# Square roots by logarithm and exponential, and a rotation whose sums TensorE makes while it transposes

## The chip, the cores and the metric

The kernel runs on one core of a Trainium2 chip, as one launch. The core has five engines that run their own instruction streams beside each other and wait for one another by semaphores: TensorE (PE, with its weight loads listed as PEld), VectorE (DVE), ScalarE (ACT), GpSimd (POOL) and SyncE (SP, which here issues transfers). Sums of matmuls are kept in PSUM, everything else in SBUF. The metric is the time of one launch on the device in microseconds (us), as the median of several runs. A profile is taken of one execution; its length is told by the span, from its first to its last instruction.

## What is computed

The reference is a network of four blocks of three layers on a small sequence x (2 batches of 128 rows, 256 wide) with a longer context (2 batches of 2048 rows). Every layer begins with a layer norm and ends with a residual sum:

```python
x = x + _L0_xattn_ref(_layernorm(x), ctx, ...)   # softmax attention over the context
x = x + _L0_attn_ref(_layernorm(x), ...)         # gated scan
x = x + _L0_ffn_ref(_layernorm(x), ...)          # mixture of 16 experts
...                                              # L1: cross attention, linear attention, soft mixture
x = x + _L2_xattn_ref(_layernorm(x), ctx, ...)   # linear attention with a sigmoid gate
...                                              # L2: rotary attention, mixture of low-rank experts
x = x + _L3_xattn_ref(_layernorm(x), ctx, ...)   # 16 heads over 2048 + 128 keys, RMS norm, rotary
x = x + _L3_attn_ref(_layernorm(x), ...)         # state-space layer
x = x + _L3_ffn_ref(_layernorm(x), ...)          # gated feed-forward with 4-bit weights
```

Two pieces matter here. The first is 1/sqrt(v + eps): in `_layernorm`, in the RMS norms of two layers and in an L2 norm. The second is the state-space layer L3_attn, with 64 heads and a state of N = 128:

```python
Bm = rmsnorm((x @ WB.T).reshape(B_, L, H, N), Bn_w) + B_bias      # Cm likewise
theta_cumsum = jnp.cumsum(theta * dt[..., None], axis=1)          # 64 angles for each head and row
Bm = rope(Bm, theta_cumsum); Cm = rope(Cm, theta_cumsum)          # x0*c - x1*s, x0*s + x1*c
...
h = a_t * h + b_t * outer(B_prev, x_prev) + g_t * outer(B_t, x_t) # scan over rows
y_t = C_t . h
```

The kernel makes the scan from products: C Bᵀ of each head (128 x 128), weighted by decays, times x.

## The kernel before

The kernel is one program of stages, a function for each layer. In most stages each operation is recorded through a small helper, `InOrder` (L219 to L227), which keeps the instructions of an engine in the order in which the program text calls them; therefore very many instructions of the profile show one line, L227, and are told apart by the names of their tiles.

**Roots.** `rstd` (L148 to L151) makes 1/sqrt(scale*v + eps) with two instructions, Sqrt on ScalarE and a reciprocal on VectorE. `norm_rows` and `layernorm` (L153 to L168) call it; `rooted` of the third block's cross attention (L1512) and `rooted` of the state-space layer (L1894) write out the Sqrt, and `rotated` (L1515) and `scaled` (L1897) the reciprocal; `l1_ffn` does it for the L2 norm (L1028). ScalarE's functions stand in tables, of which one set is active at a time; where the next function isn't in it, an instruction ACT_TABLE_LOAD stands ahead of it. Sqrt, Exp, Sin, Sigmoid and Gelu alternate all through the kernel. In l2 the gate of the cross attention is a Sigmoid (L1219) and is multiplied with 1/den later (L1268). `Tables.finish` (L313), called at L2239, takes the sines and cosines of the rotary angles of l3_xattn.

**l3_xattn** (L1430 on) goes through 8 groups of heads; keys and queries are normed and rotated by VectorE for the next group while TensorE makes the scores S and the products py of the present one.

**l3_attn** goes through 16 rounds: 8 groups of 8 heads by 2 batches. A round has, in the order in which its data flow: `angles` (projection `pt`), `stepped` (`td`, VectorE), `summed_angles` (sum over rows by a triangular matmul, TensorE), `reduced_angles` (a cast on ScalarE and a subtraction: `sc`), `sines` (Abs and two Sin, ScalarE), `decays` (`lm`, `ex`), `projected` (B and C as `pb`, two PSUM tiles of 128 x 1024, and their squares in `bc`), `squares` (two sums, `rs`), `rooted`, `scaled` (16 ScalarE multiplications `bc` <- `pb`, `rs`, one for B or C and head), `biased` (norm weight `nw` and bias `bb`: four VectorE operations of 128 x 1024), `rotated` (six VectorE operations of 128 x 1024: `t`, `ro`, `ro`, twice), `turned` (16 transposes of 128 x 128 on TensorE into four PSUM tiles, each then copied to `rT` by ScalarE), `products` (C Bᵀ, two times four matmuls), `decayed` (`m1` on VectorE, `m2` on GpSimd), `mixed` (32 matmuls with 32 columns of weights), `gated` (VectorE).

The rounds are pipelined by hand: step n of the loop at L2008 runs `decays` to `scaled` of round n, `biased` to `turned` of round n-1, `products` to `mixed` of round n-2, `gated` of round n-3 and the angles of round n+1. The order on each engine is that of the text. For one step it is

- TensorE: decays, pb (16), products of the first four heads, pt, products of the other four, angle sums, transposes, mixed;
- VectorE: bc (nw), bc (bb), gated, bc (nw), bc (bb), t, ro, ro, t, m1, ro, td, ro, m1, squares (2), reciprocal, lm, sc;
- ScalarE: a table load, ex (2), squares (2), Abs, a load, Sin (2), a load and a one-element Sqrt (`warm`, L2057), rT (4), Sqrt, cast, the 16 multiplications.

All matmuls of the layer but `pb` share four PSUM tiles (L1720). The last round is done in two halves of four heads, so `turned` is called twice there. Weights of the coming groups are fetched by SP (`weights`, L1732); the pool of single weights, `w4`, has three buffers (L2249), one each for `wx`, `wz` and, at the end, Wout.

Of the kernel before, what the change touches and what calls it, by code (L numbers as in the profile page):

```python
# [22 lines left out]
P = 128  # L23
# [12 lines left out]
class Net:  # L36


    def __init__(self, ctx, tc, ins):
# [6 lines left out]
        self.act = ctx.enter_context(tc.tile_pool(name="act", bufs=1, reuse_waits="tile"))  # L46

        c = self.const
        self.x = c.tile([P, B, D], F32, name="x")
# [90 lines left out]
    def copy(self, out, in_):  # L140
# [4 lines left out]
        else:  # L145
            self.nc.vector.tensor_copy(out, in_)

    def rstd(self, out, in_, scale, eps, act=None):  # L148
        nc = self.nc
        (act or nc.scalar).activation(out, in_, AF.Sqrt, bias=eps, scale=scale)  # L150
        nc.vector.reciprocal(out, out)  # L151

# [10 lines left out]

    def layernorm(self):
        xn = self.act.tile([P, B, D], F32, tag="xn", name="xn")
        for b in range(B):
            self.norm_rows(xn[:, b, :], self.x[:, b, :])
        return xn  # L168
# [111 lines left out]
class Tables:  # L280
# [32 lines left out]
    def finish(self):  # L313
        act = self.g.nc.scalar
        act.activation(self.cos, self.sin, AF.Abs)
        act.activation(self.cos, self.cos, AF.Sin, bias=self.g.half_pi, scale=-1.0)
        act.activation(self.sin, self.sin, AF.Sin)


# [378 lines left out]
def l0_attn(g):  # L698
# [6 lines left out]
    with tc.tile_pool(name="l0a", bufs=2, reuse_waits="tile") as p:  # L705
# [7 lines left out]
        for dc in range(2):  # L713
            ps = g.mm([P, 2, T])
            pg = g.mm([P, T])
            sl = slice(dc * P, (dc + 1) * P)
            g.project(ps[:, 0, :], lambda c: wi[:, c, sl], lambda c: xnT[:, c, :])
            g.project(ps[:, 1, :], lambda c: wf[:, c, sl], lambda c: xnT[:, c, :])
            g.project(pg, lambda c: wg[:, c, sl], lambda c: xnT[:, c, :])
            gate = p.tile([P, T], F32, tag="gate", name="gate")  # L720
            act.activation(gate, ps[:, 1, :], AF.Sigmoid)
            nc.gpsimd.memset(gate[:, P:P + 1], 0.0)
            om = p.tile([P, T], F32, tag="om", name="om")
            act.activation(om, ps[:, 1, :], AF.Sigmoid, scale=-1.0)
            v = p.tile([P, T], F32, tag="v", name="v")
            act.activation(v, ps[:, 0, :], AF.Sigmoid)
            nc.vector.tensor_tensor(v, v, ps[:, 0, :], ALU.mult)
            nc.vector.tensor_tensor(v, v, om, ALU.mult)
            o = p.tile([P, T], F32, tag="o", name="o")
            nc.vector.tensor_tensor_scan(o, gate, v, 0.0, ALU.mult, ALU.add)  # L730
            nc.gpsimd.tensor_tensor(osq[:, dc, :], o, o, ALU.mult)
            sg = p.tile([P, T], F32, tag="sg", name="sg")
            act.activation(sg, pg, AF.Sigmoid)
            if dc:
                g.mixing.decays(act)
            nc.vector.tensor_tensor(sg, sg, pg, ALU.mult)
            nc.vector.scalar_tensor_tensor(yT[:, dc, :], o, gn[:, dc:dc + 1], sg, ALU.mult, ALU.mult)
# [134 lines left out]
def l1_mixing(g, ctxT):  # L872
# [6 lines left out]
    with tc.tile_pool(name="l1x", bufs=2, reuse_waits="tile") as p:  # L879
        mix, dd = g.mixing, g.mixing.dd  # L880
        act = InOrder(tc, nc.scalar)

        def normed(b, n):
# [104 lines left out]
def l1_ffn(g, mu, b1):  # L988
# [6 lines left out]
    with tc.tile_pool(name="l1f", bufs=2, reuse_waits="tile") as p:  # L995
# [21 lines left out]
        for b in range(B):  # L1017
# [9 lines left out]
            nc.scalar.activation(xu[:, b, :], xl[:, b, :], AF.Square, accum_out=n2)  # L1027
            nc.scalar.activation(n2, n2, AF.Sqrt)  # L1028
            nc.vector.tensor_scalar(n2, n2, 1e-12, None, ALU.max)
            nc.vector.reciprocal(n2, n2)  # L1030
            nc.vector.tensor_scalar(xu[:, b, :], xl[:, b, :], n2, sc, ALU.mult, ALU.mult)
# [84 lines left out]
        def hidden(ep):  # L1116
# [7 lines left out]
            nc.vector.tensor_tensor(hv, ph[:, :, :, 0:H], rz.unsqueeze(3).to_broadcast([P, 2, B, H]), ALU.mult)  # L1124
            nc.scalar.activation(hv, hv, AF.Gelu)

# [23 lines left out]
def l2(g, ctxT, codes, last):  # L1150
# [9 lines left out]
    with tc.tile_pool(name="l2", bufs=1, side="right", reuse_waits="tile") as p:  # L1160
# [8 lines left out]
        wkv, wq, wg = (g.load("L2_xattn_" + k) for k in ("Wkv", "Wq", "Wg"))  # L1169
        bg = mine("bg", [P, 2], g.ins["L2_xattn_bg"], pc)  # L1170
        wxo = mine("wxo", [P, 2, D], g.ins["L2_xattn_Wo"], pc)
        wqk, wv, wo = (g.load("L2_attn_" + k) for k in ("Wqk", "Wv", "Wo"))
# [33 lines left out]
        def context_attention(px, b):  # L1206
# [11 lines left out]
            for dc in range(2):  # L1218
                nc.scalar.activation(gate[:, dc, :], ps[:, 1, dc, :], AF.Sigmoid, bias=bg[:, dc:dc + 1])  # L1219
            yield  # L1220
# [36 lines left out]
            den = px.tile([P, 2, P], F32, tag="den", name="den", bufs=1)  # L1257
            nc.vector.tensor_scalar(den, pn[:, 1], 1e-6, None, ALU.add)
            pk = g.mm([P, 2, P])
# [6 lines left out]
            for c in range(2):  # L1266
                nc.tensor.matmul(pn[:, 0, c, :], lhsT=kvb[:, c, :], rhs=q[:, c, :], start=True, stop=True)
            nc.vector.tensor_tensor(den, den, gate, ALU.mult)  # L1268
            oT = px.tile([P, 2, P], F32, tag="oT", name="oT", bufs=1)
# [160 lines left out]
def l3_xattn(g, ctxT, cos, sin, values):  # L1430
# [12 lines left out]
    with ExitStack() as ctx:  # L1443
# [18 lines left out]
        class Group:  # L1462
# [49 lines left out]
            def rooted(self, lo, hi):  # L1512
                act.activation(self.rs[:, lo:hi], self.rs[:, lo:hi], AF.Sqrt, bias=g.eps6, scale=1.0 / HD)

            def rotated(self, lo, hi):  # L1515

                kq, rot, b = self.kq, self.rot, self.b
                n = hi - lo
                dve.reciprocal(self.rs[:, lo:hi], self.rs[:, lo:hi])
                dve.tensor_tensor(kq[:, lo:hi, :], kq[:, lo:hi, :], self.rs[:, lo:hi].unsqueeze(2).to_broadcast([P, n, HD]), ALU.mult)  # L1520
# [191 lines left out]
def l3_attn(g):  # L1712
# [5 lines left out]
    with tc.tile_pool(name="l3w", bufs=2, reuse_waits="tile") as pw, tc.tile_pool(name="l3a", bufs=1, reuse_waits="tile") as p, tc.tile_pool(name="l3t", bufs=2, reuse_waits="tile") as p2, \  # L1718
            tc.tile_pool(name="l3aps", bufs=1, space=PSUM, reuse_waits="tile") as g.ps:
        def mm(shape=(P, 512)):  # L1720
            return g.ps.tile(list(shape), F32, tag="mm", name="mm", bufs=4)
# [6 lines left out]
        nc.sync.dma_start(nw, g.ins["L3_attn_BCn_w"].partition_broadcast(P))  # L1728

        late = p.tile([P, 4, P], BF16, name="late")  # L1730
        nc.vector.memset(late, 0.0)
# [94 lines left out]
        class Round:  # L1826
# [67 lines left out]
            def rooted(self):  # L1894
                act.activation(self.rs, self.rs, AF.Sqrt, bias=g.eps6, scale=1.0 / N)

            def scaled(self, parts=(slice(0, HG),)):  # L1897
                dve.reciprocal(self.rs, self.rs)
                for hs in parts:
# [9 lines left out]
            def rotated(self, hs=slice(0, HG)):  # L1909

                nh = hs.stop - hs.start
                e1, e2 = self.bc[:, :, hs, 0:64], self.bc[:, :, hs, 64:128]
                sb, cb = (self.sc[:, i, hs].unsqueeze(1).to_broadcast([P, 2, nh, 64]) for i in range(2))
                if hs.start == 0:
                    self.ro = p2.tile([P, 2, HG, N], F32, tag="ro", name="ro", bufs=1)
                r1, r2 = self.ro[:, :, hs, 0:64], self.ro[:, :, hs, 64:128]
                for r, x, y, op in ((r1, e1, e2, ALU.subtract), (r2, e2, e1, ALU.add)):
                    t1 = p2.tile([P, 2, HG, 64], F32, tag="t1", name="t1", bufs=1)[:, :, 0:nh, :]
                    dve.tensor_tensor(t1, y, sb, ALU.mult)
                    yield  # L1920
                    dve.tensor_tensor(r, x, cb, ALU.mult)
                    yield
                    dve.tensor_tensor(r, r, t1, op)
                    yield

            def turned(self, halves=(0, 1)):
                if 0 in halves:
                    self.rT = p2.tile([P, 2, HG, P], F32, tag="rT", name="rT")
                for n in halves:
                    for a in range(2):  # L1930
                        tp = mm([P, 4, P])
                        for i in range(4):
                            pe.transpose(tp[:, i, :], self.ro[:, a, 4 * n + i, :], g.ident)
                        act.copy(self.rT[:, a, 4 * n:4 * n + 4, :], tp)
# [42 lines left out]
        halves = (slice(0, HG // 2), slice(HG // 2, HG))  # L1977
        warm = g.sm([P, 1], "warm")
        rounds = {n: Round(*todo[n]) for n in range(2)}
# [20 lines left out]
        reduced = second.reduced_angles()  # L2000
        next(reduced)
        first.sines()
        first.decays()
        second.decay_inputs()
# [3 lines left out]
        for n in range(1, len(todo) + 3):  # L2008
# [47 lines left out]
            if now:  # L2056
                act.activation(warm, g.eps6, AF.Sqrt)  # L2057
            if rot and n - 1 < last:
# [81 lines left out]
def l3_ffn(g, codes, out):  # L2140
# [4 lines left out]
    with tc.tile_pool(name="l3sc", bufs=1, reuse_waits="tile") as psc, tc.tile_pool(name="l3f", bufs=1, reuse_waits="tile") as p, tc.tile_pool(name="l3d", bufs=2, reuse_waits="tile") as p2, \  # L2145
# [27 lines left out]

        xn = g.layernorm()
        tp = g.ps.tile([P, 2, B, P], F32, tag="up", name="tp", bufs=3)
# [40 lines left out]
def tile_perceiver(ctx: ExitStack, tc: tile.TileContext, ins, out: bass.AP):  # L2216
# [3 lines left out]
    with tc.tile_pool(name="w", bufs=1, reuse_waits="tile") as g.w, tc.tile_pool(name="ctxT", bufs=1, reuse_waits="tile") as pc, tc.tile_pool(name="l3t", bufs=1, reuse_waits="tile") as pt, \  # L2220
# [4 lines left out]
        with g.psum():  # L2225
            with tc.tile_pool(name="l1s", bufs=1, reuse_waits="tile") as pm:
# [4 lines left out]
                with tc.tile_pool(name="beside", bufs=1, reuse_waits="tile") as tmp:  # L2231
                    slots, tables = Slots(g, pm, tmp), Tables(g, pt, tmp)
                    ex = gate_spread(g, tmp)
                    l0_attn(g)
                    l0_ffn(g, itertools.chain(slots.steps(), [None] * 6, tables.steps()), ex)
                l1_mixing(g, ctxT)
                mixed.close()
                l1_ffn(g, slots.mu, slots.b1)
            tables.finish()  # L2239
            codes = Codes(g, ctx.enter_context(tc.tile_pool(name="codes", bufs=1, side="right", reuse_waits="tile")))  # L2240
# [7 lines left out]
    with tc.tile_pool(name="w_end", bufs=1, reuse_waits="tile") as g.w:  # L2248
        g.w_bufs = {"w2": 1, "w4": 3, "row": 1}  # L2249
        l3_attn(g)  # L2250
# [126 lines left out]
```

## Time and profile before

| | |
|---|---|
| median of 3 runs | 1529.2 us (1528.87 to 1530.35) |
| the profiled execution | 1534.16 us |
| its span | 1532.4 us |
| mean granted clock of TensorE | 0.917 |
| busy: PE, DVE, ACT, POOL | 1389.1, 1121.8, 812.5, 141.3 us |
| l3_xattn, about | 700 to 1130 us |
| rounds of l3_attn | from about 1150 to 1460 us, 19.2 us each in the steady part |
| table loads shown at L227 | 72, 1283 ns each |

Two numbers of time stand side by side: the profiled execution took 1534.16 us, of which the span covers 1532.4, and the runs without a profile have a median of 1529.2. A line of groups reads: line, engine, operation, tile written <- tiles read, shape, count | busy time in all, mean ns of one | idle time of the engine just before them, and what ended it. A line of the timeline reads: start, length, engine, line, operation, tiles, shape and count. A line of the chain reads: start, length, what the end was waiting for then. Matmuls overlap: the length of one record is longer than the distance from one to the next.

### The profile page before, as it was taken

How to read it: one execution, taken by the hardware profiler on the slowest of the kernel's cores; microseconds unless marked ns; L12 is line 12 of the kernel's file. 1: busy time of each engine (PE TensorE's matmuls, PEld its weight loads, DVE VectorE, ACT ScalarE, POOL GpSimd, SP SyncE). 2: the span in 40 equal slices, each digit the busy share in tenths (PEclk: the TensorE clock that was granted, in tenths of full speed). 3: DMA queues.
4: the chain of work that ended last, by engine and by line, in shares of the span. 5: the costliest groups of instructions: out<-in, count | busy, mean ns of one | idle time of the engine just before them, and what ended most of it. 6: DMA issues, size and time to landing. Idle time of an engine off the chain costs nothing.

```text
span 1532.4 us, 18453 instructions
## 1 busy us (share of the span) xinstructions
PE 1389.1 (91%) x6936; PEld 852.2 (56%) x6936; DVE 1121.8 (73%) x1970; ACT 812.5 (53%) x1251; POOL 141.3 (9%) x140
## 2 busy tenths in 40 slices
PE   8859997799989999989999999999888999999878
PEld 5413333677456786655666656665444555555557
DVE  6889997576256476675776776777537999999876
ACT  3567776333232433353554455455448888888721
POOL 6620001011000000000000000000000111111110
PEclk9955555999999999989999999999999999999989
DMA  7799999754250342412001000000152222221110
GB/s 189 137 177 204 204 201 197 222 167 146 75 170 9 96 139 65 121 42 69 29 0 55 29 6 37 28 28 0 36 198 81 92 96 97 96 97 42 35 35 7
DMA packets 225140, 143.87 MB, mean 94 GB/s; under 512 B 177897, under 2 KB 203770, under 8 KB 220699
## 3 DMA queue, kind: packets, MB, share of 16 engines
q1 hardware_dynamic: 221696, 140.75, 35.4%
q10 hardware_dynamic: 3290, 1.77, 0.5%
q8 instruction: 55, 0.90, 0.2%
q0 software_dynamic: 64, 0.18, 0.1%
q14 instruction: 35, 0.28, 0.1%
HBM read 90.33 MB, written 8.65 MB: 65 GB/s over the span
## 4 chain that ended last, share of the span: by engine, by line
PE 55%; DVE 27%; ACT 9%; DMA 4%; issue 3%; POOL 2%; DVEq 0%; SPq 0%; ACTq 0%; POOLq 0%
PE mm L184 9%; PE wide L227 9%; PE py L227 8%; DVE S L227 7%; PE mm L227 6%; PE tr L227 5%; DVE bc L227 4%; DVE ro L227 4%; DMA pT<-Si 2%; ACT bc L227 2%; PE acc L1235 2%; PE sc L227 2%; PE acc L227 2%; DVE t L227 1%; DVE rs L227 1%
## 5 line engine op out<-in xcount | busy, mean ns | idle before, releaser
L227 DVE TENSOR_SCALAR_CACHE_REDUCE S<-sc 128x1024 f32<-128x1024 f32 x128 | 150.4, 1219 | 6.9 <-PE sc L227 3.6
L227 PE MATMUL py<-pT,v 128*128 128x512 f32 x272 | 141.1, 605 | 9.5 <-ACT pT L227 9.5
L227 PE MATMUL sc<-kT,qT 48*128 48x512 bf16 x256 | 130.0, 614 | 19.7 <-DMA kT<-kpad 6.5
L227 ACT ACTIVATE Si<-S,nb,sq 128x4096 int16<-128x4096 f32 (+1 forms) x35 | 122.7, 3506 | 42.8 <-issue 27.8
L227 ACT COPY pT<-tr 128x512 f32<-128x512 f32 x136 | 78.7, 584 | 82.7 <-PE tr L227 82.7
L227 PE MATMUL wide<-kT,qT 128*128 128x512 f32 x256 | 116.7, 599 | 0.0
L227 ACT ACTIVATE S<-S,nb 128x2176 f32<-128x2176 f32 x32 | 67.5, 2108 | 92.5 <-DVE nb L227 92.5
L227 PE MATMUL pb<-wb,xT 128*128 128x512 f32 x256 | 112.6, 592 | 0.0
L227 PEld LDWEIGHTS tr<-ident,S 128*128 128x128 f32 x544 | 67.5, 141 | 68.4 <-issue 37.7
L227 DVE TENSOR_SCALAR_CACHE_REDUCE S<-wide 128x1024 f32<-128x1024 f32 x64 | 77.7, 1223 | 27.9 <-PE wide L227 27.5
L227 ACT ACT_TABLE_LOAD x72 | 92.4, 1283 | 3.2 <-PE mm L227 1.2
L227 PEld LDWEIGHTS <-pT 128*128 128x128 bf16 x1024 | 36.5, 105 | 94.7 <-issue 87.8
L227 PE MATMUL tr<-ident,S 128*128 128x128 f32 x544 | 81.4, 274 | 3.4 <-ACT S L227 3.3
L227 PEld LDWEIGHTS pb<-wb,xT 128*128 128x128 f32 x256 | 48.9, 191 | 59.9 <-issue 55.6
L227 PEld LDWEIGHTS wide<-kT,qT 128*128 128x128 f32 x256 | 47.4, 193 | 50.4 <-issue 43.6
L227 ACT ACTIVATE bc<-pb,rs 128x128 f32<-128x128 f32 x256 | 67.8, 424 | 0.9 <-DVE rs L227 0.9
L227 ACT ACTIVATE bc<-pb 128x1024 f32<-128x1024 f32 x32 | 32.8, 1025 | 49.3 <-PE pb L227 49.3
L184 PE MATMUL mm<-wvs,ctxT 128*128 128x512 f32 x116 | 57.0, 614 | 0.0
L227 PE MATMUL wide<-w,ctxT 128*128 128x128 f32 x448 | 53.0, 277 | 2.6 <-DVE S L227 2.6
L227 PEld LDWEIGHTS wide<-w,ctxT 128*128 128x128 f32 x448 | 51.1, 192 | 3.9 <-DVE S L227 3.9
L1952 POOL TENSOR_SCALAR_AFFINE_SELECT m<-m 128x512 f32<-128x512 f32 x32 | 33.1, 1035 | 213.8 <-DVE m L227 213.8
L227 PE MATMUL mm<-xT,w 128*128 128x256 f32 x216 | 50.8, 379 | 0.0
(540 smaller groups left out, 2851.7 us busy)
## 6 DMA issues: line engine op xcount, KB each, us to landing
w<-in_L_ffn_w_dram SPq DMA_DIRECT2D x25, 384.0 KB
vs<-st SPq DMA_DIRECT2D x32, 256.0 KB
v<-vs SPq DMA_DIRECT2D x8, 1024.0 KB
wb<-in_L_attn_WB_dram SPq DMA_DIRECT2D x8, 1024.0 KB
wb<-in_L_attn_WC_dram SPq DMA_DIRECT2D x8, 1024.0 KB
bb<-in_L_attn_BC_bias_dram SPq DMA_DIRECT2D x8, 1024.0 KB
ctxT<-in_ctxT_dram SPq DMA_DIRECT2D x15, 512.0 KB
w<-in_ctx_dram SPq DMA_DIRECT2D x8, 512.0 KB
```

Source lines behind the costliest of these rows:

```text
L184: self.nc.tensor.matmul(out, lhsT=lhsT(c), rhs=w(c), start=(c == 0), stop=(c == n - 1))
L227: return lambda *a, **k: self.tc.keep_in_program_order(f(*a, **k))
L1235: nc.tensor.matmul(acc[c], lhsT=kf[:, i, c * P:(c + 1) * P], rhs=cx[:, t % 4 + i, :], start=(t + i == 0), stop=(t + i == NT - 1))
L1952: nc.gpsimd.affine_select(out=self.m2[:, ns, :], in_=self.m1[:, ns, :], pattern=[[0, 4], [1, P]], compare_op=ALU.is_ge, fill=0.0, base=-1, ...
```

## The change

It has two parts.

The first replaces 1/sqrt by exp(-0.5 ln(v)): Ln and Exp, both on ScalarE, without a reciprocal, and loads by hand, at a few places, the table set that holds both functions. The sigmoid gate of l2 becomes an Exp whose 1 + exp(-x) is multiplied into the denominator. The sines of `Tables.finish` are made in steps inside l0_ffn. The number of table loads in the program goes from 101 to 43; three in a steady round of l3_attn become two.

The second splits the rotation of l3_attn. VectorE still multiplies both halves of `bc` by the cosine (two operations of 128 x 1024). For the first four heads it also finishes the second half of the vector, for the other four the first half (a product `t1` and a sum, 128 x 512 each). The remaining sine product goes to a tile `kt` of its own and is not added by VectorE: `turned` adds it. It makes each transpose of 128 x 128 as two matmuls against the identity, 64 columns of weights each, and a third, of `kt` against the identity or its negative (`minus`), accumulates into one of the two halves. The two tiles of the heads' halves are filled alternately, and both are copied when both are done. TensorE's order is otherwise as before. VectorE's order between the bias and m1 becomes ro, ro, t1, ro, t1, ro, m1, kt, td, kt. The weight pool w4 has two buffers.

```diff
+    def exp_and_log(self):
+
+        self.tc.keep_in_program_order(self.nc.scalar.preload_act_table_set("natural_log_exp_and_others"))
+
     def rstd(self, out, in_, scale, eps, act=None):
-        nc = self.nc
-        (act or nc.scalar).activation(out, in_, AF.Sqrt, bias=eps, scale=scale)
-        nc.vector.reciprocal(out, out)
+
+        act = act or self.nc.scalar
+        act.activation(out, in_, AF.Ln, bias=eps, scale=scale)
+        act.activation(out, out, AF.Exp, scale=-0.5)
...
     def finish(self):
-        act = self.g.nc.scalar
+        act = InOrder(self.g.tc, self.g.nc.scalar)
         act.activation(self.cos, self.sin, AF.Abs)
+        yield
         act.activation(self.cos, self.cos, AF.Sin, bias=self.g.half_pi, scale=-1.0)
+        yield
         act.activation(self.sin, self.sin, AF.Sin)
+        yield
...
-                nc.scalar.activation(gate[:, dc, :], ps[:, 1, dc, :], AF.Sigmoid, bias=bg[:, dc:dc + 1])
+                nc.scalar.activation(gate[:, dc, :], ps[:, 1, dc, :], AF.Exp, bias=bg[:, dc:dc + 1], scale=-1.0)
+            nc.vector.tensor_scalar(gate, gate, 1e30, 1.0, ALU.min, ALU.add)
...
-            nc.vector.tensor_scalar(den, pn[:, 1], 1e-6, None, ALU.add)
+            nc.vector.scalar_tensor_tensor(den, pn[:, 1], 1e-6, gate, ALU.add, ALU.mult)
...
-            nc.vector.tensor_tensor(den, den, gate, ALU.mult)
...
             def rooted(self, lo, hi):
-                act.activation(self.rs[:, lo:hi], self.rs[:, lo:hi], AF.Sqrt, bias=g.eps6, scale=1.0 / HD)
+                g.rstd(self.rs[:, lo:hi], self.rs[:, lo:hi], 1.0 / HD, g.eps6, act)
...
             def rotated(self, hs=slice(0, HG)):
...
-                r1, r2 = self.ro[:, :, hs, 0:64], self.ro[:, :, hs, 64:128]
-                for r, x, y, op in ((r1, e1, e2, ALU.subtract), (r2, e2, e1, ALU.add)):
-                    t1 = p2.tile([P, 2, HG, 64], F32, tag="t1", name="t1", bufs=1)[:, :, 0:nh, :]
-                    dve.tensor_tensor(t1, y, sb, ALU.mult)
...
+                dve.tensor_tensor(self.ro[:, :, hs, 64:128], self.bc[:, :, hs, 64:128], cs_, ALU.mult)
+                yield
+                dve.tensor_tensor(self.ro[:, :, hs, 0:64], self.bc[:, :, hs, 0:64], cs_, ALU.mult)
+                yield
+                for n, hp, sb in sides:
+                    t1 = p2.tile([P, 2, HG // 2, 64], F32, tag="t1", name="t1", bufs=1)
+                    dve.tensor_tensor(t1, self.bc[:, :, hp, lanes[n]], sb, ALU.mult)
+                    ro = self.ro[:, :, hp, lanes[1 - n]]
+                    dve.tensor_tensor(ro, ro, t1, ALU.subtract if n else ALU.add)
                     yield
+                for n, hp, sb in sides:
+                    dve.tensor_tensor(self.kt[:, :, hp, :], self.bc[:, :, hp, lanes[1 - n]], sb, ALU.mult)
                     yield
...
-                for n in halves:
-                    for a in range(2):
-                        tp = mm([P, 4, P])
-                        for i in range(4):
-                            pe.transpose(tp[:, i, :], self.ro[:, a, 4 * n + i, :], g.ident)
+                for a in range(2):
+                    tps = [mm([P, HG // 2, P]) for _ in parts]
+                    for i in range(HG // 2):
+                        for n, tp in zip(parts, tps):
+                            for k in range(2):
+                                r = slice(64 * k, 64 * k + 64)
+                                pe.matmul(tp[r, i, :], lhsT=self.ro[:, a, 4 * n + i, r], rhs=g.ident, start=True, stop=(k != n))
+                        for n, tp in zip(parts, tps):
+                            pe.matmul(tp[64 * n:64 * n + 64, i, :], lhsT=self.kt[:, a, 4 * n + i, :], rhs=signed[n], start=False, stop=True)
+                    for n, tp in zip(parts, tps):
                         act.copy(self.rT[:, a, 4 * n:4 * n + 4, :], tp)
...
             if now:
-                act.activation(warm, g.eps6, AF.Sqrt)
+                g.exp_and_log()
...
-        xn = g.layernorm()
+        act = InOrder(tc, nc.scalar)
+        xn = g.layernorm(act)
+        act.preload_act_table_set("exp_and_others")
...
-                    l0_ffn(g, itertools.chain(slots.steps(), [None] * 6, tables.steps()), ex)
+                    l0_ffn(g, itertools.chain(slots.steps(), [None] * 6, tables.steps(), tables.finish()), ex)
...
-        g.w_bufs = {"w2": 1, "w4": 3, "row": 1}
+        g.w_bufs = {"w2": 1, "w4": 2, "row": 1}
```

## The prediction

> **What bounds the kernel now.** I read the page first, then busy time by stage, then the chain of waits through one round of the state-space layer, the timeline beside it, and the groups kept apart by shape for prices.
>
> ```profile
> span 1532.4 us, 18453 instructions
> ...
> PE 1389.1 (91%) x6936; PEld 852.2 (56%) x6936; DVE 1121.8 (73%) x1970; ACT 812.5 (53%) x1251; POOL 141.3 (9%) x140
> ...
> PE 55%; DVE 27%; ACT 9%; DMA 4%; issue 3%; POOL 2%; DVEq 0%; SPq 0%; ACTq 0%; POOLq 0%
> ...
> L227 ACT ACT_TABLE_LOAD x72 | 92.4, 1283 | 3.2 <-PE mm L227 1.2
> ```
>
> TensorE is busy 91% and makes 55% of the chain that ends last; ScalarE is 53% busy, so most of its table loads, 1.283 us each, should stand in time that nobody waits for. A removed load counts only where the chain passes through it. Next, one steady round of l3_attn by busy time (columns: length, then busy time of PE, PEld, DVE, ACT, POOL, granted clock, DMA share, GB/s):
>
> ```profile
> 1218.41:1237.63 19.22, 17.68 (x96) 10.29 (x94) 18.05 (x20) 15.91 (x34) 3.23 (x4) 1.00 0.24 83
> ```
>
> Of 19.22 us VectorE works 18.05 and TensorE 17.68: neither has room for three more microseconds. Who waits for whom stands in the chain (start, length, what):
>
> ```profile
> 1232.23 0.61 DVE td L227
> 1232.84 0.14 issue
> 1232.98 1.10 PE mm L227 x2
> 1234.07 0.04 issue
> 1234.11 0.64 PE mm L227 x4
> 1234.75 0.02 issue
> 1234.77 2.05 ACT rT L227 x4
> 1236.83 0.02 issue
> 1236.85 0.31 ACT rs L227
> 1237.16 0.47 ACT sc L227
> 1237.63 2.08 ACT bc L227 x8
> ```
>
> The round is a loop through three engines. VectorE works from the first `bc` product (1220.52 in the timeline) to the end of `td` (1232.84): 12.32 us. TensorE sums the angles and turns `ro`; ScalarE copies the four turned tiles to `rT`, takes the root, casts, and makes eight multiplications, after which VectorE starts the next round's `bc` at 1239.74: 6.90 us. 12.32 + 6.90 = 19.22. So `turned` and its copies stand on the path that sets the end, and the three loads of the round (1222.56, 1230.30, 1232.84) do not: ScalarE sits idle 2.41 us for the projection behind them.
>
> **Part one: the rotation.** The prices:
>
> ```profile
> 510.48 0.66 PE L1131 MATMUL mm<-cT,h 128*64 128x128 f32 x8
> 521.68 0.88 PE L1131 MATMUL mm<-cT,h 128*64 128x128 f32 x12
> 1234.11 1.97 PE L227 MATMUL mm<-ident,ro 128*128 128x128 f32 x16
> 1236.00 1.94 PE L227 MATMUL mm<-m,xb 128*32 128x128 f32 x32
> L227 DVE TENSOR_TENSOR ro<-ro,t 128x1024 f32<-128x1024 f32 x28 | 34.5, 1231 | 0.5
> L227 DVE TENSOR_TENSOR rot<-rot,t 128x512 f32<-128x512 f32 x14 | 9.7, 692 | 0.5
> ```
>
> *TensorE.* One matmul lasts 0.27 in the records, but they follow one another faster. The new shape (64 columns of weights, 128 of moving data, float32) exists in l1_ffn: 8 in 0.66, 12 in 0.88, so (0.88 - 0.66)/4 = 0.055 each; the 32-column ones of `mixed` take (1.94 - 0.27)/31 = 0.054. Transposes take (1.97 - 0.27)/15 = 0.113. Sixteen transposes become 96 matmuls: 96 x 0.055 = 5.28 where 1.97 stood, +3.3 us of TensorE per round. No row has a sum in place over two operands of this shape; the upper end is the full-width rate, 0.11 x 96 = 10.6, the lower one 0.02 each (if tiles overlapped more than any row shows), 1.9. I take 0.055, the row with the same shape.
>
> *VectorE.* Up to `td` five operations of 1024 elements (t, ro, ro, t, ro: 4.80 from 1225.62 to 1230.42 and 1.13 after `m`) become two of 1024 (2.40) and five of 512 at 0.62 (step between starts) to 0.69 (mean): 5.5 to 5.85, so 0.1 to 0.4 less; I take 0.25. After `td`, one of 1024 becomes one of 512 (`kt1`), 0.55 less, but that is beside TensorE's angle sum (1.10), which begins at once: nothing on the path. The two `kt` products run before TensorE asks for them.
>
> *PSUM and the copies.* Before, a tile is copied while the next is turned: from the first transpose to the end of the last copy 2.72. After, two tiles are filled alternately, so nothing can be copied until 48 matmuls, 2.64, are done. Four buffers serve all of `mm`; the fourth tile needs the first tile back, that is its copy: it starts 0.21 after the tile's last matmul (1234.77 against 1234.11 + 4 x 0.113) and is 0.51 long (2.05/4), so it ends at about 3.35, when TensorE has stood since 2.75: a stall of 0.6. Then 46 more, 2.53, to 5.88; then 0.2 less a pitch and two copies, 1.03: 7.0. That is **+4.3** on the path. The bounds of the stall are 0 and 0.7.
>
> *Root.* Sqrt (0.31, next instruction 0.21 after its start) becomes Ln and Exp: +0.2 on ScalarE. The reciprocal that goes (0.25 on VectorE) stood beside the cast.
>
> Per round -0.25 + 4.3 + 0.2 = **+4.2**, a period of about 23.4. What is late next: with pb, angle sums, products and `mixed` TensorE's own work is about 17.5 + 3.3 = 20.8, still under 23.4, so the loop decides and not the sum. Fifteen rounds turn in full: 15 x 4.2 = 63. The last turns in two halves of 48: 2 x 1.6 more on TensorE, at a lower clock, less about 0.7 each on VectorE: +2. Sum for the layer: **+65**.
>
> The smaller weight pool (w4: 3 to 2 buffers) makes Wout's load on SP wait until wx or wz is free. Behind it on SP stand only loads whose tiles are freed later still (the bias load of the next weights is issued at 1225.61); Wout is needed after the last round. Nothing; its price without that cover is a load's few us, once.
>
> **Part two: square roots without Sqrt.** 101 loads in the program become 43. Where they are on the chain: l3_xattn, once between two groups:
>
> ```profile
> 784.77 2.20 ACT S L227 x2
> 786.97 0.02 issue
> 786.99 0.86 ACT L227
> 787.84 0.44 issue
> 788.28 0.30 ACT rs L227
> 788.58 0.48 ACT pT L227
> ```
>
> The load and what follows it (0.86 + 0.44 = 1.30) go, Exp adds 0.2: -1.1, and TensorE's wait for pT (1.32 us at 789.11) shrinks by it. Seven groups have a successor: -8. The other load of a group lies before a 3.5 us wait for VectorE's `nb`: nothing. In l2, three loads (529.01, 645.71, 675.95) are on the chain: 3 x (1.28 - 0.2) = -3. The new gate there swaps a Sigmoid for Exp and a VectorE step off the path: between -0.3 and +0.7, taken as 0. Against it: the Sin tables are now finished in order inside l0_ffn, where other ScalarE work queues behind their Sin (about +1), and l3_ffn's preload stands before the xT copy (between 0 and 1.3, taken 0.3). Other removed loads stood in ScalarE's idle time. Sum: **-10**. Bounds: 0, were all hidden anyway, and -20, were the loads of l0 and l1 also on the path.
>
> On the price of a load, the row says 1.283 us, and the next instruction starts at once (load at 1230.30, Sin at 1231.59). The Trainium skill, "ScalarE: Activation LUTs", section "What ACT_TABLE_LOAD costs", states about 1283 ns plus a drain of about 1380 ns, 2.66 us for each switch; no such drain is seen after this load. By that page alone the 58 removed loads would be worth an estimated 154 us and the change a large gain.
>
> **Sum.** +65 - 10 = +55. The profiled execution took 1534.16 (span 1532.4 and 1.76 around it); it would become about 1589. It lies 4.96 above the median of the runs, so I forecast 1529.2 + 55 = **1584**.
>
> **Rivals.**
> 1. *TensorE's sum, not the loop, decides.* If VectorE or ScalarE work slid past the longer turn (say the copies of the first two tiles overlap better and `bc` starts earlier), the round would be 20.8 to 21: +1.6 x 15 = 24, +2, -10: 1545. Against it: every engine's order is fixed by hand, and the eight multiplications stand behind the copies on ScalarE.
> 2. *Narrow matmuls cost as much as wide ones here*, because accumulating pairs cannot overlap: 0.11 x 96 = 10.6. The loop grows by about 5.3 more: 15 x 9.5 + 4 - 10 = +136, 1665. Against: the l1_ffn row.
> 3. *The other side: faster, because the loads cost more than the chain lets see.* 58 go, 16 of them in the rounds. Were all 58 on the path at the row's 1.283, part two would be -74 instead of -10, and the kernel -9: 1520. It decides when a removed load is worth 65/58 = 1.12 us on average. For it: the chain is one execution's, and ScalarE hands work to both other engines in every stage. Against it: in the round shown ScalarE waits 2.41 us after its loads, and over the span it is idle 47%.
> 4. *Narrow tiles overlap further than any row shows*, at 0.02 each. Turn and copies then take about 94 x 0.02 + 2.0 = 3.9, where 2.0 is two waits of 0.2 and the three copies that nothing hides; the round grows by 1.1: 16 - 10 = +6, 1535. Only at 0.013 would it be lost in the measurement. Against: no narrow row is under 0.054.
>
> **How the numbers follow.** Forecast 0.75 (its own range 1562 to 1602: stall 0 to 0.7, part two 0 to -20); rival 1 0.07; rival 2 0.06; rival 3 0.07; rival 4 0.05, of which 0.02 within the measurement. The range takes in the forecast's spread and reaches to rival 1: 1545 to 1604; rivals 2, 3 and 4, 0.18, stay out. A difference of 0.2%, 3 us, is about what a measurement can tell from none. Faster 0.07, within 0.2% 0.02, slower 0.91.
>
> **What would show it.** Right: the 96 matmuls of a round in 5.3 us with a gap of some 0.6 near the middle; the first rT copy 2.8 us after the first of them; rounds of 23 to 24 us; VectorE idle some 5 us a round, mostly before `sc` or `bc`, both waiting for ScalarE; the stretch between l3_xattn groups 1 us shorter. Wrong: a turn of 2 us, or of 10; rounds of 21 with TensorE full; stages before l3_attn shorter by more than 20.

## The result and the profile after

The changed kernel takes 1590.55 us (median of 4 runs, 1588.01 to 1592.79), the kernel before 1529.78 (4 runs): a ratio of 1.0383, 95% interval 1.0364 to 1.0403. That is 60.8 us slower; 1590.55 is 6.5 above the forecast of 1584 and inside the range. Between the two profiled executions (1534.16 and 1588.01) the difference is 53.9.

First the page of the changed kernel. Its helper stands at L233.

```profile
span 1586.3 us, 20976 instructions
...
PE 1448.7 (91%) x8216; PEld 906.9 (57%) x8216; DVE 1096.9 (69%) x1939; ACT 744.7 (47%) x1239; POOL 126.9 (8%) x140
...
PE 58%; DVE 26%; ACT 8%; DMA 3%; issue 3%; POOL 2%; SPq 0%; DVEq 0%; ACTq 0%; POOLq 0%
```

VectorE and ScalarE work 25 and 68 us less than before, as the change intends; TensorE works 60 us more, about what the time grew by, but the sum alone doesn't tell why. One steady round by busy time (length, then PE, PEld, DVE, ACT, POOL, clock, DMA share, GB/s):

```profile
1264.41:1288.27 23.86, 21.50 (x173) 13.71 (x172) 17.40 (x20) 14.52 (x33) 2.14 (x4) 1.00 0.21 67
```

TensorE is 21.50 busy and the round is 23.86: it is not TensorE's sum alone that decides. The chain of waits through the same round tells what does (start, length, what):

```profile
1276.23 0.61 DVE td L233
1276.84 0.14 issue
1276.98 3.92 PE mm L233 x50
1280.89 0.57 ACT rT L233
1281.47 0.04 issue
1281.51 2.67 PE mm L233 x44
1284.18 1.05 ACT rT L233 x2
1285.24 0.21 ACT rs L233
1285.45 0.02 issue
1285.47 0.21 ACT rs L233
1285.69 0.47 ACT sc L233
1286.16 2.08 ACT bc L233 x8
1288.25 0.02 issue
1288.27 1.24 DVE bc L233
```

It is the loop of before, longer in one place: the angle sum and the first two tiles, 3.92; a copy on which TensorE's next tile waits, 0.57; the other two tiles, 2.67; then the two copies that nothing covers, 1.05; then two short instructions for the root where there was one. The same stretch as TensorE's timeline, at the third matmul of two heads, one in each column half (the 64 columns of weights fill the lower or the upper half of the tile's partitions):

```profile
1278.49 0.27 PE L233 MATMUL mm<-minus,kt 128*64 128x128 f32 x1
1278.50 0.27 PE L233 MATMUL mm<-ident,kt 128*64 128x128 f32 x1
1278.60 0.27 PE L233 MATMUL mm<-minus,kt 128*64 128x128 f32 x1
1278.61 0.27 PE L233 MATMUL mm<-ident,kt 128*64 128x128 f32 x1
```

Each matmul of the code is two records ("passes" from here on): 48 matmuls are 96 passes, while a transpose is one. Two passes in different halves start 0.01 apart, two in the same half 0.11. So 0.055 a pass is half of 0.11, and holds only while the halves alternate. The Trainium skill, "TensorEngine Tiling (Array Packing)", section "Key Properties", states that different tiles can execute in parallel; the trace agrees, with 0.01 us between their starts. A transpose in float32 is one record where a matmul is two: 16 transposes were 16 records in the kernel before.

Where the time went, by marks in the traces (us). The last three rows are lengths. Thirteen of the fifteen full turns lie between the first and the last `td`; the third row holds the other two and the two halves of the last round:

| | before | changed | difference |
|---|---|---|---|
| first `td` of l3_attn starts | 1142.1 | 1127.8 | -14.3 |
| first to last `td` | 284.5 | 341.0 | +56.5 |
| last `td` to last copy to `rT` | 46.3 | 54.0 | +7.7 |
| last copy to `rT` to the end | 59.5 | 63.5 | +4.0 |

For the experiments one number is used throughout: the **period**, the distance between the starts of `td` in successive steady rounds. Two values alternate in every run (19.23 and 19.60 before), and the mean of the two is given: 19.41 before, 23.67 after, +4.26.

### The profile page after: what moved, and what is told of

It reads as the page before. It is cut to its first block, busy times and chain, and to the rows that moved or that the text cites. A ratio compares the mean times of both kernels' runs of the same rounds, so it can differ in the third digit from the quotient of the medians.

```text
span 1586.3 us, 20976 instructions
## 1 busy us (share of the span) xinstructions
PE 1448.7 (91%) x8216; PEld 906.9 (57%) x8216; DVE 1096.9 (69%) x1939; ACT 744.7 (47%) x1239; POOL 126.9 (8%) x140
## 3 DMA queue, kind: packets, MB, share of 16 engines
q8 instruction: 65, 1.06, 0.3%
## 4 chain that ended last, share of the span: by engine, by line
PE 58%; DVE 26%; ACT 8%; DMA 3%; issue 3%; POOL 2%; SPq 0%; DVEq 0%; ACTq 0%; POOLq 0%
PE mm L233 11%; PE mm L190 9%; PE wide L233 8%; DVE S L233 8%; PE py L233 8%; PE tr L233 5%; DVE bc L233 4%; DVE ro L233 3%; ACT bc L233 2%; PE acc L1250 2%; DMA pT<-Si 2%; ACT rT L233 2%; PE sc L233 1%; PE one L233 1%; PE acc L233 1%
## 5 line engine op out<-in xcount | busy, mean ns | idle before, releaser
L233 DVE TENSOR_SCALAR_CACHE_REDUCE S<-sc 128x1024 f32<-128x1024 f32 x128 | 150.6, 1219 | 7.1 <-PE sc L233 3.9
L233 PE MATMUL sc<-kT,qT 48*128 48x512 bf16 x256 | 130.0, 614 | 20.6 <-DMA kT<-kpad 6.4
L233 ACT ACTIVATE Si<-S,nb,sq 128x4096 int16<-128x4096 f32 (+1 forms) x35 | 122.7, 3506 | 44.5 <-issue 28.1
L233 PE MATMUL py<-pT,v 128*128 128x512 f32 x272 | 140.7, 603 | 1.7 <-ACT pT L233 1.7
L233 PE MATMUL wide<-kT,qT 128*128 128x512 f32 x256 | 116.8, 600 | 0.0
L233 ACT COPY pT<-tr 128x512 f32<-128x512 f32 x136 | 78.9, 586 | 80.3 <-PE tr L233 80.3
L233 ACT ACTIVATE S<-S,nb 128x2176 f32<-128x2176 f32 x32 | 67.5, 2108 | 103.6 <-DVE nb L233 103.6
L233 PE MATMUL pb<-wb,xT 128*128 128x512 f32 x256 | 113.9, 598 | 1.8 <-ACT bc L233 1.8
L233 PEld LDWEIGHTS tr<-ident,S 128*128 128x128 f32 x544 | 67.7, 142 | 68.0 <-issue 37.1
L233 DVE TENSOR_SCALAR_CACHE_REDUCE S<-wide 128x1024 f32<-128x1024 f32 x64 | 77.7, 1223 | 28.1 <-PE wide L233 27.9
L233 PE MATMUL mm<-ident,ro 128*64 128x128 f32 x1024 | 86.4, 281 | 7.8 <-ACT rT L233 6.3
L233 PEld LDWEIGHTS <-pT 128*128 128x128 bf16 x1024 | 36.6, 106 | 95.3 <-issue 85.3
L233 PEld LDWEIGHTS pb<-wb,xT 128*128 128x128 f32 x256 | 47.5, 190 | 65.5 <-issue 51.3
L233 PE MATMUL tr<-ident,S 128*128 128x128 f32 x544 | 81.5, 274 | 3.5 <-ACT S L233 3.3
L233 ACT COPY rT<-mm 128x512 f32<-128x512 f32 x64 | 34.6, 589 | 104.5 <-PE mm L233 104.5
L233 PEld LDWEIGHTS mm<-ident,ro 128*64 128x64 f32 x1024 | 63.4, 140 | 23.5 <-issue 12.9
L233 PEld LDWEIGHTS wide<-kT,qT 128*128 128x128 f32 x256 | 47.3, 192 | 50.5 <-issue 43.5
L233 ACT ACTIVATE bc<-pb,rs 128x128 f32<-128x128 f32 x256 | 67.8, 422 | 0.1
L233 DVE TENSOR_TENSOR sc<-mm,sc 128x512 f32<-128x512 f32 x16 | 11.0, 690 | 69.6 <-ACT sc L233 69.6
L233 ACT ACTIVATE bc<-pb 128x1024 f32<-128x1024 f32 x32 | 32.7, 1023 | 54.3 <-PE pb L233 54.3
L233 DVE TENSOR_TENSOR bc<-bc,nw 128x1024 f32<-128x1024 f32 (+1 forms) x34 | 39.3, 1157 | 24.3 <-ACT bc L233 24.1
```

What stands on the lines that cost most here:

```text
L233: return lambda *a, **k: self.tc.keep_in_program_order(f(*a, **k))
```

## The experiments

The theory was that the turn and its late copies, standing on the loop, cost the time, and that the roots bring a little elsewhere. The rivals were that Ln and Exp lengthen the loop, that the loads are worth more than the chain shows, that every narrow pass costs 0.055 wherever it lies, and that VectorE's saving is a real gain that the turn eats up.

**The roots alone.** The changed kernel with `rotated` and `turned` of the kernel before.

> The changed kernel with the old rotation and the old sixteen transposes: only the roots, the gate, the sine tables and the loads are as changed. Theory (the loss is all in the turn and its late copies): a round takes 19.2 to 19.5 (0.2 for Exp, nothing else), the stages up to l3_xattn keep their 14 us, the last layer its 4 us of loss, so 1517 to 1525 where the kernel before has 1529.8. Rival one (Ln and Exp lengthen the loop as well): rounds of 20 or more, 1535 to 1545. Rival two (the removed loads are worth what their rows show in the rounds too): rounds of 18, about 1500.

Measured: 1527.2, 0.9968 of the kernel before (0.9954 to 0.9983). The period is 19.66, +0.25, so Ln and Exp cost what was said and no more. The first `td` starts at 1126.4, about as in the changed kernel. The end, 66.0 us from the last copy to `rT`, is 6.5 longer than before. The theory stands; the total is 2 us above its span, and the tail asks for a run of its own (below).

**The rotation alone.** The kernel before with the new `rotated`, `turned` and weight pool.

> The kernel before with the new rotation and turn alone, Sqrt and reciprocal kept. Theory: the two parts add up; a round takes 23.6 (23.86 less 0.26 for Exp), the layer loses 60 to 66 and nothing is won elsewhere: 1588 to 1598. Rival (the third table load of a round now collides with the late copies): rounds of 24.5 or more, 1605 and above.

Measured: 1590.31, ratio 1.0385 (1.0355 to 1.0416); period 23.43, +4.02 over before. The parts add up: 4.02 + 0.25 = 4.27, and 4.26 was measured with both. The first `td` starts at 1136.9, though nothing ahead of it was changed: so 5.2 of the 14.3 in the table need not be the change's, and about 9 remain. That is known to some 4 us only: among the eight profiled executions with the changed stages ahead of l3_attn and early tables (the changed kernel and seven of the runs here) this start varies from 1126.4 to 1130.5.

**The third matmul left out.** The kt products are made by VectorE and not added.

```diff
-                        for n, tp in zip(parts, tps):
-                            pe.matmul(tp[64 * n:64 * n + 64, i, :], lhsT=self.kt[:, a, 4 * n + i, :], rhs=signed[n], start=False, stop=True)
```

> The changed kernel without the third matmul of each head (the product kt is made but never added, so the rotation is incomplete): 64 passes of 64 columns for a turn instead of 96, in the same order, both tiles of a pair copied when both are full. Theory: 32 passes x 0.055 = 1.76 less on the loop, rounds of 21.9 on average where the changed kernel has 23.67. Rival (the accumulating matmuls are hidden or cost double): 23.5 or 20.2.

Measured: period 21.53, 2.14 less; 1552.59 in one run. 32 x 0.055 = 1.76 of it is the passes. The rest goes with the copies: without the third matmul the first tile of a pair is full four passes before the second, so in each pair its copy starts some 0.2 earlier, and TensorE's wait for the returned tile falls from 0.45 to 0.25. The accumulating passes are neither hidden nor dear.

**The same, tile by tile.** Each tile is copied while the next is filled.

```diff
-                for a in range(2):
-                    tps = [mm([P, HG // 2, P]) for _ in parts]
-                    for i in range(HG // 2):
-                        for n, tp in zip(parts, tps):
+                for n in parts:
+                    for a in range(2):
+                        tp = mm([P, HG // 2, P])
+                        for i in range(HG // 2):
...
+                        act.copy(self.rT[:, a, 4 * n:4 * n + 4, :], tp)
```

> As the run without the third matmul, but the four tiles are filled one after the other and each is copied while the next is filled. Theory (two halves alternate in every tile now, so the rate stays at 0.055 a pass, and the copies hide but for the last): 64 x 0.055 + 0.7 = 4.2 from the first matmul to the last copy's end, rounds 2.9 under the changed kernel's 23.67, 20.8; the run without the third matmul has 21.5, so the late copies alone are worth 0.7. Rival (copies are no part of the loss): 21.5 again.

Measured: period 20.79, 1533.06 in one run. In its timeline the 64 passes run without a stop and the copies follow them:

```profile
1261.92 3.71 PE L233 MATMUL mm<-ident,ro 128*64 128x128 f32 x64
1263.06 0.59 ACT L233 COPY rT<-mm 128x512 f32<-128x512 f32 x1 [1.89 <-PE mm L233]
1263.93 0.59 ACT L233 COPY rT<-mm 128x512 f32<-128x512 f32 x1 [0.29 <-PE mm L233]
1264.81 0.59 ACT L233 COPY rT<-mm 128x512 f32<-128x512 f32 x1 [0.29 <-PE mm L233]
1265.68 0.59 ACT L233 COPY rT<-mm 128x512 f32<-128x512 f32 x1 [0.29 <-PE mm L233]
```

From the first pass to the root at 1266.16 it is 4.24. The late copies alone are worth 21.53 - 20.79 = 0.74 a round.

**The same, with transposes.** `pe.transpose` of each head's `ro` in place of the two narrow matmuls: the changed VectorE work beside the old TensorE work, with kt still not added.

> As the run before it in this list, with the sixteen full transposes of the kernel before in place of the 64 passes (kt is made and not added, the rotation is incomplete): all of the changed VectorE work, none of the changed TensorE work. Theory (VectorE's shorter work is worth next to nothing, since the part of it on the loop is no shorter): rounds of 19.3 to 19.7, beside 19.66 of the run with the roots alone. Rival (the shorter VectorE work is a real gain that the turn eats up): rounds of 18.8 or less.

Measured: period 19.03, 1511.12 in one run. This lies between the two expectations, nearer to the rival: against the run with the roots alone (19.66) VectorE's shorter work is worth 0.63 a round. The theory gave VectorE too little. By the timelines of the two runs, the stretch from VectorE's first `bc` to the end of `td` is 0.27 shorter, the turn starts 0.20 earlier after `td`, and from there to the root it is 0.19 shorter (0.03 is lost behind it). The turn itself is as in the kernel before, but the root waits for more than the copies: in the kernel before it starts 0.04 after VectorE's two sums end, 3.98 after the end of `td`.

```profile
1234.48 2.33 DVE L227 TENSOR_REDUCE rs<-bc 128x8 f32<-128x1024 f32 x2
...
1236.85 0.31 ACT L227 ACTIVATE rs<-rs,eps 128x16 f32<-128x16 f32 x1
```

Here the operation between `td` and the sums is half as long, the sums end 3.46 after `td` (1273.82), and the root starts 0.17 behind them:

```profile
1274.90 1.93 PE L233 MATMUL mm<-ident,ro 128*128 128x128 f32 x16
...
1274.94 2.34 DVE L233 TENSOR_REDUCE rs<-bc 128x8 f32<-128x1024 f32 x2
...
1277.45 0.34 ACT L233 ACTIVATE rs<-rs,eps 128x16 f32<-128x16 f32 x1
```

In the changed kernel the sums end at 1280.28 and the root starts at 1285.12, so there this part of the saving is covered by the longer turn.

**All tiles one by one, with the third matmul.** The order of the run before last, with kt added after the two matmuls of each head.

> The changed kernel, with the four tiles of the turn filled one after the other and each copied at once; the same matmuls. Theory (a pass of 64 columns occupies its own column half for 0.11, and two halves run beside each other only when the order alternates them): four of six passes of a tile now fall on one half, so the turn takes 16 x 4 x 0.11 = 7.0 instead of 5.3 plus a stall of 0.5, the copies hide but for the last 0.7: 7.7 from the first matmul to the last copy's end instead of 7.1, rounds of 24.5, 1597 to 1602. Rival (each pass costs 0.055 wherever it lies): turn 5.3, 6.0 with the last copy, rounds of 22.8, 1573 to 1577.

Measured: period 24.11, 0.44 above the changed kernel; 1591.82, ratio 1.0387 (1.0356 to 1.0417), which can't be told from the changed kernel's. The total thus missed the theory's span, but the turn itself, 7.56 from its first pass to the root, is near the theory's 7.7 and excludes the rival's 6.0. In the timeline the pattern of one head returns every 0.44:

```profile
1282.86 0.44 PE L233 MATMUL mm<-ident,ro 128*64 128x128 f32 x4
1283.13 0.27 PE L233 MATMUL mm<-minus,kt 128*64 128x128 f32 x1
1283.14 0.32 PE L233 MATMUL mm<-ident,ro 128*64 128x128 f32 x1
1283.24 0.27 PE L233 MATMUL mm<-minus,kt 128*64 128x128 f32 x1
1283.30 0.43 PE L233 MATMUL mm<-ident,ro 128*64 128x128 f32 x3
1283.57 0.27 PE L233 MATMUL mm<-minus,kt 128*64 128x128 f32 x1
```

The sum of a tile always goes to the same half, which gets four of six passes: 4 x 0.11 = 0.44 a head, where the alternating order needs 6 x 0.055 = 0.33. Sixteen heads took 6.97 (1282.86 to `mixed` at 1289.83). Better hidden copies and slower passes nearly cancel.

**Late tables.** The roots alone, with the sines of l3_xattn made after l1_ffn as in the kernel before.

```diff
-                    l0_ffn(g, itertools.chain(slots.steps(), [None] * 6, tables.steps(), tables.finish()), ex)
+                    l0_ffn(g, itertools.chain(slots.steps(), [None] * 6, tables.steps()), ex)
...
+            for _ in tables.finish():
+                pass
```

> As the run with the roots alone, but the sine tables are made where the kernel before makes them, after l1_ffn. Theory (the Sin steps put into l0_ffn delay its end, by 3.4 us between the starts of l0_attn's output and the last expert sum): 2 to 3.5 faster than the run with the roots alone. Rival (that shift is something else, or what is won is lost at the tables' old place): within 1 us of it.

Measured: 1593.34, ratio 1.0398 (1.0372 to 1.0425), 66 slower than the roots alone. Both expectations fell. ScalarE's timeline in l3_xattn has the reason:

```profile
915.54 1.28 ACT L233 ACT_TABLE_LOAD   x1
916.83 0.30 ACT L233 ACTIVATE rs<-rs,eps 128x8 f32<-128x8 f32 x1
917.15 1.28 ACT L233 ACT_TABLE_LOAD   x1
918.44 0.21 ACT L233 ACTIVATE rs<-rs 128x8 f32<-128x8 f32 x1
```

After the last Sin nothing loads the shared set by hand any more, and now Ln and Exp each fetch a set of their own, at every root: 22 loads between 760 and 1100, where the run with the roots alone has none. The products py span 424.4 us there instead of 383.1. One more line after the tables tests this:

```diff
+            g.exp_and_log()
```

> The run with the late tables (1593), with one more instruction: the set that holds Ln and Exp is loaded by hand after the last Sin of the tables. Theory (without it Ln and Exp of l3_xattn each fetch a set of their own, 22 loads in 340 us where the roots-only run has none): back at the roots-only run, 1524 to 1530. Rival (the position of the Sin steps costs it): 1580 or more.

Measured: 1530.63, ratio 1.0000 (0.9983 to 1.0017), 0.6 above the theory's span and far below the rival's; py spans 382.7. The missing load was the cause. The Trainium skill, "ScalarE: Activation LUTs", section "Table sets: the hidden batching unit", states that ln and then exp need one load, since one set has both; in this run they took two, until that set was loaded by hand. The guess that the Sin steps in l0_ffn had cost 3.4 us is dropped: the stretch from l0_attn's output to l0_ffn's last expert sum varies from 92.0 to 99.9 among the profiled executions, and the kernel with the old l0 code (the rotation alone) is at 93.6.

**The head of l3_ffn.** The roots alone, with the layer norm of l3_ffn called as in the kernel before and no load by hand behind it.

```diff
-        act = InOrder(tc, nc.scalar)
-        xn = g.layernorm(act)
-        act.preload_act_table_set("exp_and_others")
+        xn = g.layernorm()
```

> As the run with the roots alone, but l3_ffn begins as in the kernel before: its layer norm out of the hand-kept order and no table load by hand. Theory (the head changes the order in which the recorded operations of l3_ffn are laid out; from the last copy to rT to the end the roots-only run took 66.0 where the kernel before took 59.5): the tail is back at 60 to 61, 4 to 6 faster than the roots-only run, 0.7% under the kernel before, about 1520. Rival (the tail's loss comes from Ln and Exp themselves or from the granted clock): within 1.5 of the roots-only run.

Measured: 1523.44, 0.9952 of the kernel before (0.9934 to 0.9970); the interval overlaps that of the roots alone. The end, 63.7 us from the last copy to `rT`, is 2.3 shorter than there and not back at 60 to 61: the theory's span is missed, and the rival, a lower granted clock, is not excluded for the rest. From the first product of l3_ffn (`pg`) to the end it is 48.46 in the kernel before, 52.11 in the changed kernel and with the roots alone, and 49.91 here. What the order does is seen ahead of TensorE's last eight products with `wd`, in the changed kernel and then in the kernel before:

```profile
1579.70 2.78 PE L2235 MATMUL acc<-wd,t 128*128 128x256 f32 x8 [2.38 <-DVE t L2230]
```

```profile
1526.64 1.99 PE L2208 MATMUL acc<-wd,t 128*128 128x256 f32 x8 [0.78 <-DVE t L2203]
```

The three lines of the head change the order of the operations in all of l3_ffn. In the changed kernel the chain goes at last through 4 us of ScalarE and VectorE steps (1575.6 to 1579.7), and TensorE stands still for 2.38 of them, where it waits 0.78 for one step in the kernel before; with the roots alone the wait is 2.39, here 0.78. So 1.6 us are the order's. The other 2 of the 3.7 went with the clock: it was 0.75 up to the first product with `wd` and 0.93 behind it in the changed kernel, 0.86 and 1.00 in the kernel before; and the run with the late tables, which has the changed head at a clock of 1.00 in both, takes 48.52. Whether the order also brings the lower clock was not tested.

**The cast first.** The run just told, with the next round's cast ahead of the copies to `rT`, where ScalarE was idle.

```diff
+            reduced = iter(())
+            if nxt:
+                reduced = nxt.reduced_angles()
+                next(reduced)
             if rot and n - 1 < last:
                 rot.turned()
...
-            reduced = iter(())
-            if nxt:
-                reduced = nxt.reduced_angles()
-                next(reduced)
```

> As the run before it in this list, and in a round ScalarE makes the cast of the next round's angles ahead of the four copies to rT instead of between the root and the sixteen multiplications. Theory (the loop runs through ScalarE's copies, root, Exp, cast and multiplications; ScalarE is idle 0.4 before the copies): 0.4 per round less, rounds of 19.2 instead of 19.66, 6 faster: about 1514. Rival (the cast delays the copies by as much as it leaves later): same within 1.5.

Measured: period 19.32 (0.34 less), 1519.71, 0.9914 of the kernel before (0.9895 to 0.9933): faster than both kernels of the case. The total is 3.7 under the run before it, less than the 6 of the theory. In its chain the cast is gone from between root and multiplications:

```profile
1257.07 2.05 ACT rT L233 x4
1259.13 0.02 issue
1259.15 0.32 ACT rs L233
1259.46 0.02 issue
1259.49 0.22 ACT rs L233
1259.71 0.02 issue
1259.73 2.19 ACT bc L233 x8
```

The +4.26 of a round, step by step, each from one difference of periods:

| step | from | us a round |
|---|---|---|
| Exp behind Ln | 19.66 - 19.41 | +0.25 |
| VectorE's shorter work | 19.03 - 19.66 | -0.63 |
| 64 narrow passes for 16 transposes | 20.79 - 19.03 | +1.76 |
| both tiles of a pair copied late | 21.53 - 20.79 | +0.74 |
| the third matmul, 32 passes | 23.67 - 21.53 | +2.14 |

## Why the prediction was right, and which terms were mis-sized

- *What bounds the kernel.* Right: the loop through VectorE, the turn and ScalarE's copies decides, not TensorE's sum (21.50 of 23.86). Rival 1 is excluded by that, rivals 2 and 4 by the 0.055 of alternating passes, rival 3 by the roots-only run.
- *The terms of a round.* The timelines give the loop in the forecast's own stretches (means of the steady rounds, us):

| | before | roots alone | transposes, kt not added | changed |
|---|---|---|---|---|
| VectorE's first `bc` to the end of `td` | 12.50 | 12.50 | 12.23 | 12.23 |
| to the first pass of the turn | 1.28 | 1.28 | 1.08 | 1.18 |
| to the root | 2.74 | 2.74 | 2.55 | 7.12 |
| to the first multiplication | 0.68 | 0.93 | 0.96 | 0.94 |
| to VectorE's next `bc` | 2.21 | 2.21 | 2.21 | 2.21 |

- *The turn, +4.3.* Measured +4.38: the stretch from the first pass to the root was forecast at 7.0 and is 7.12 (1278.00 to 1285.12); the stall, forecast at 0.6, is 0.45; the first copy, forecast 2.8 after the first pass, starts 2.87 after it. What was forecast as "96 matmuls" are 96 passes of 48.
- *VectorE, -0.25.* Measured -0.27. What it does after `td` was put at nothing; the turn starts 0.10 earlier. *Root, +0.2.* Measured +0.26. Sum: +4.2 forecast, +4.26 measured. The table of steps adds up to the same, but there VectorE's -0.63 stands against a loop that still has the short turn.
- *Fifteen rounds, 63.* From the first `td` to the root behind the last full turn the changed kernel takes 61.8 more (371.4 against 309.7). In this some luck cancels: two rounds of the changed execution ran at a lower clock, +3.2 (last section); in the kernel before the last full turn did, 16 transposes in 3.66 us at a clock of 0.50, so that round lost only 1.0; and the first turned round, still start-up, lost 1.5.
- *The last round, +2.* Measured +2.4, from that root to the last copy, but not by the forecast's parts: it took 0.055 a pass, +1.6 for each half. A turn of one half fills one tile at a time, so its sums always fall on one column half, as in the tile-by-tile run: 8 x 0.44 = 3.5 us for a half, and the chain has 3.50 for the second one (1519.30 to 1522.80), where the kernel before needed 1.06. So TensorE's part is +2.4 and not +1.6; VectorE's work ahead of it fell by 0.9 where 0.7 was forecast. Both kernels had part of the round at a lower clock.
- *The layer, +65.* Measured 61.8 + 2.4 = 64.2.
- *Part two, -10.* About -9 up to l3_attn (-14.3 less the 5.2 that the execution of before was late), known to some 4 us. Most of it is l3_xattn, as forecast: py spans 381.5 instead of 388.8, -7.3 where -8 stood. But l3_ffn, costed at +0.3, lost 3.7, of which 1.6 by its order and the rest with the clock; there the price was sought in one table load, and not in what a new call does to a stage whose order nobody wrote down.
- *The smaller weight pool, nothing.* Not tested by itself. The rotation alone has it, and from its last copy to `rT` to the end it takes 60.7 where the kernel before takes 59.5.
- *From the execution to the median.* The sum, +55, fits the profiled executions (+53.9), in part by luck: the 5.2 by which the execution of before was late at l3_attn stands in the -14.3 and about offsets the 3.7 lost in l3_ffn. Against the medians (+60.8) it is 5.8 short: the execution of before lay 4.4 above its median of four, that of after 2.5 below. What of this belongs to which stage no trace shows.

## What to carry to other kernels

Count work handed from VectorE to TensorE in passes and not in matmuls: here a float32 transpose is one pass of 0.11, a narrow float32 matmul two passes of 0.055 that hold only while the column halves alternate, and the saving on VectorE was worth 0.4 to 0.6 a round against some 4.5. Then look whether the receiving engine stands on the loop, and when its results can be fetched: two tiles filled alternately are both late. A gain from fewer table loads is counted only where the chain passes through them, and it hangs on which set stands loaded when the pair of functions is reached.

## What the runs showed of the hardware that was not expected

Two of the steady rounds of the changed kernel last 25.5 instead of 23.5 to 23.9. In one of them the granted clock is 0.63 while the first pair of tiles is turned:

```profile
1348.90:1353.20 4.30, 4.30 (x51) 4.25 (x52) 3.34 (x3) 0.00 (x0) 0.64 (x1) 0.63 0.04 15
```

Eight passes take 1.12 there instead of 0.66. TensorE had waited 1.91 us for `td` just before, but it waits as long in rounds that keep their full clock, so the wait alone doesn't explain it; without the third matmul, three intervals are 1.4 to 1.6 longer than their like in the one order, and none in the other; and the old turn has them too, with the roots alone one interval is 21.07 instead of 19.85, at a clock of 0.69 from 1236.5 to 1242.0. The Trainium skill, "TensorE: Matmul & The Clock Gate", section "Part 1: The HAM clock gate", describes a free-running activity window, with whose phase the number of slow matmuls varies from run to run. That two rounds are hit and not all would fit it, but no run here tests it.
